# Two-layer graph-attention and mixture-of-experts kernel: x of five pairs beside layer 0's last blocks, and the last stage of tiles 0 to 11 beside layer 1's last blocks

## The chip, the core and the metric

The kernel runs on one NeuronCore of a Trainium2 chip. Its time is the device time of one execution, in microseconds. A core has five engines with a queue each: PE multiplies matrices (PEld is its loading of weights), DVE and ACT work on vectors, POOL does too and issues the indirect DMAs, and SP issues the other DMAs. All DMAs run on the core's 16 DMA engines. An engine does its instructions in their order; an instruction that waits holds up all behind it on that engine.

## The reference, cut to what matters

x has 2708 rows of 256 numbers. Each of two layers adds first an attention over the graph `adj` and then a mixture of experts, in which each row goes to its two best of 8 (layer 0) or 16 (layer 1) experts:

```python
x = x + gnn0(layernorm(x), adj)           # softmax attention over the neighbours
x = x + ffn0(layernorm(x))                # 8 experts, 256 -> 1024 -> 256, gelu, top 2
x = x + gnn1(layernorm(x), adj)           # hyperbolic attention
n = layernorm(x)
x = x + (layernorm(n + moe1(n)) * gamma + beta)   # 16 experts, 256 -> 512 -> 256, relu, top 2
```

All four parts depend on all rows of the part before, so each seam between two of them is a place where work can run dry.

## The kernel before

The rows are in 22 tiles (20 of 128 rows and two of 74), handled as 11 pairs. The kernel is one program with all loops unrolled. The orders of PE, ACT, DVE and SP are written out by the kernel itself, POOL's order is set by the compiler's scheduler.

**Experts.** In both layers the rows are sorted into blocks of 128 rows of one expert, 47 blocks in layer 0 (`SURE0`) and 45 in layer 1 (`SURE1`). For a block, SP loads the expert's w1 and w2 into one of three rooms (1 MB each in layer 0, 0.5 MB each in layer 1; a load is skipped where the room already holds the expert) and fetches the block's rows from `rows_d`. PE turns the rows (`tr_ps`), multiplies by w1 (`hid_ps`), ACT applies the function, PE multiplies by w2 (`out_ps`), DVE scales by the gate's weight (`yo`), and POOL adds the result to the rows' tokens in HBM with an indirect DMA (`add`). There are two sums in HBM, `sums[0]` for even blocks and `sums[1]` for odd ones; each add to a sum waits until the one before it on that sum has landed. `sums[0]` starts with x itself (layer 0) or its normalized rows (layer 1). Layer 0's blocks are ordered by `Experts.run`: per block it issues w1 of block b+2, the hidden products, the turn of b+1, the output of b-1, w2 of b+2, the rows of b+3, the weight of b (`weigh`: DVE `side`, ACT tanh), and then calls `beside(b)`. Layer 1's blocks are ordered by `Experts.stream`, in which generators ask a planner (`Clock`) for stretches of engine time, written as `yield "DVE", 0.7`; the planner decides by these planned times in which order the instructions are written. A `Mark` is a planned moment, `Slots` stand for a ring of buffers.

The first blocks of each layer (24 in layer 0, `EARLY0`) are full pages of the tokens of the first tiles; a page that is open then comes among the next E blocks, E being the number of experts. So all rows of the first tiles are complete after a known block.

**The seam between the layers.** After layer 0's last block, `project1` runs for each pair, paced by `Turns`: SP reads the pair's rows from both sums into `h_all` and `xp`, POOL adds them (L1468), SP keeps the sum in `x_d` for later, DVE computes mean and variance (L421, L422), ACT and DVE the root, DVE applies it (`xr`, L437), PE turns the pair (`tr_ps`, L455), ACT copies it (`xts`) and squares its rows (`norms`, L1496), PE multiplies by `w1x` (`u_ps`, L460), ACT copies the result to `h_all`. The attention of layer 1 follows.

**The end.** In layer 1, `add_beta` makes POOL add a column and beta to x1 (two operations a tile, L1854 and L1855). After the last block `load_y` reads all 22 tiles from both sums into `y_all` (which lies over `mask_t`), in the groups 2, 2, 4, 4, 4, 4, 2. `last1` adds the two sums on PE (`y_ps`, L1894), DVE computes mean and variance, ACT and DVE the root, ACT applies it (L446), and `out_rows` multiplies by gamma on POOL (L1914), adds x1 on DVE (L1918) and stores to `out`.

Of the kernel before, what the change touches and what calls it, by code (L numbers as in the profile page):

```python
# [146 lines left out]
def kernel(  # L147
# [72 lines left out]
    def row_tile(name, bufs):  # L220
        return row.tile([P, D], F32, name=name, tag=name, bufs=bufs)
# [26 lines left out]

    room_scope = ExitStack()
# [6 lines left out]
    def xn_tile():  # L256
        return keep0.tile([P, RW], F32, name="xn", bufs=4)
# [16 lines left out]

    x_all = keep0.tile([P, T, D], F32, name="x_all")
# [431 lines left out]
    class Experts:  # L707
# [5 lines left out]
        def __init__(self, layer, router, w1, b1, w2, func, sums, tags, xg, xt, bias, sure):  # L713
            self.layer, self.router, self.w1, self.w2 = layer, router, w1, w2
            self.func, self.sums, self.b1 = func, sums, b1
            self.t_tag, self.h_tag, self.o_tag = tags
            self.xg_tile, self.xt_tile, self.bias_tile = xg, xt, bias
            E, _, self.F = w1.shape
            self.FC, self.NB = self.F // P, router.blocks
            self.rooms, self.rows, self.known, self.planned, self.stages = {}, {}, 0, 0, []  # L720
            self.last_add, self.adds = {}, []
            self.b1_rows = w1x.rearrange("p c f -> p (c f)")[:E, :self.F]
            self.taken, self.sure = taken_of[layer], sure
# [177 lines left out]
        def add(self, b, yo):  # L901
            k = b % 2
            ins = nc.gpsimd.indirect_dma_start(  # L903
                out=self.sums[k][:, :], in_=yo, in_offset=None,
                out_offset=bass.IndirectOffsetOnAxis(ap=self.rows.pop(b)[:, D:D + 1].bitcast(I32),
                                                     axis=0), compute_op=OP.add)
            if k in self.last_add:
                tc.add_manual_dep(ins.ins, self.last_add[k].name, LANDED, reason="the same rows")
            self.last_add[k] = ins.ins
            if k == 0:  # L910
                self.adds.append(ins.ins)
# [6 lines left out]
        def store(self, t, r, src):  # L918

            ins = nc.sync.dma_start(self.sums[0][t * P:t * P + r, :], src)  # L920
            for other in self.adds:
                tc.declare_no_dep(ins.ins, other, reason="other tokens' rows")

# [12 lines left out]
        def stream(self, clock, stages, bank, acc, xrs, los, wides, widened, started):  # L936
# [3 lines left out]
                {upto: Mark() for upto in stages} for _ in range(3))  # L940
            hidden_at, out_at, xg_at, xt_at, ht_at, w_at = (
# [67 lines left out]
            def finish(b, ps, slot):  # L1009
                yield "DVE", 0.7  # L1010
                yo = self.scaled(b, ps, weights.pop(b))
                clock.set(slot)
                yield "POOL", 1.6
                self.add(b, yo)
                clock.set(xr_slots.pop(b))

# [213 lines left out]
    def close0(pair, ahead, behind, last=False):  # L1230
# [19 lines left out]
        for t, r in pair:  # L1250
            router0.rows[t] = keep0.tile([P, RW], F32, name="xr", bufs=5)
            ln_f0.apply(router0.rows[t][:r, :D], x_all[:r, t, :], t, r)
            yield 1
# [137 lines left out]

    with tc.tile_pool(name="experts0", bufs=1) as late0:
        room = late0.tile([P, 4096], F32, name="room2")
        experts0.add_room(2, room[:, :2048], room[:, 2048:])
        l1_weights = []

        def combine(b):
            if b == EARLY0 + 2:
                l1_weights.extend(load_combined(late0))
            if b == EARLY0 + 4:  # L1400
                combine_weights(*l1_weights)

        experts0.run(late0, turns, (2, 1, 2), combine)
# [6 lines left out]
    h_all = side.tile([P, T, D + 1], F32, name="h_all1")  # L1410
# [24 lines left out]
    ln_a1 = Norm("a1")  # L1435
    c0, scale, p_all, p_scale = kept("c0", 1.0), kept("scale"), kept("p_all"), kept("p_scale")
    norms = kept("norms", 1.0, 2 * T).rearrange("p (k t) -> p k t", k=2)

    def fetch_rows(tl, src, group):

        full = [t for t, r in group if r == P]
        if full:
            lo = full[0] * P
            nc.sync.dma_start(tl[:, :len(full)], src[lo:lo + len(full) * P, :].rearrange(  # L1444
                "(t p) d -> p t d", p=P))
        if len(full) < len(group):
            nc.sync.dma_start(tl[:TAIL, len(full):], src[TF * P:W, :].rearrange(
                "(t p) d -> p t d", p=P)[:TAIL])

    x_d = dram.tile([W, D], F32, name="x_d")  # L1450

    def keep_rows(src, pair):
        if pair[1][1] == P:
            lo = pair[0][0] * P
            nc.sync.dma_start(x_d[lo:lo + 2 * P, :].rearrange("(t p) d -> p t d", p=P), src)
        else:
            for q, (t, r) in enumerate(pair):
                nc.sync.dma_start(x_d[t * P:t * P + r, :], src[:r, q])

    def project1(pair):  # L1460

        xa = h_all[:, pair[0][0]:pair[0][0] + 2, :D]
        xb = side.tile([P, 2, D], F32, name="xp", bufs=4)
        fetch_rows(xa, sums0[0], pair)
        fetch_rows(xb, sums0[1], pair)
        yield 3
        if pair[1][1] == P:
            nc.gpsimd.tensor_tensor(xa, xa, xb, OP.add)  # L1468
        else:
            for q, (t, r) in enumerate(pair):  # L1470
                nc.gpsimd.tensor_tensor(xa[:r, q], xa[:r, q], xb[:r, q], OP.add)
# [8 lines left out]
        xp = [side.tile([P, RW], F32, name="xr", bufs=13)[:, :D] for _ in pair]  # L1480
        for q, (t, r) in enumerate(pair):
            ln_a1.apply(xp[q][:r], xa[:r, q], t, r)
        yield 1
        ps = ps_tile("tr_ps", "tr").rearrange("p (t c n) -> p t c n", c=DC, n=P)
# [10 lines left out]
        for q, (t, r) in enumerate(pair):  # L1495
            nc.scalar.activation(row_tile("junk", 4)[:r, 1:], xp[q][:r, 1:], AF.Square,  # L1496
                                 accum_out=norms[:r, 0, t:t + 1])
# [83 lines left out]
    widen(0, 1)  # L1581
    widen(1, 1)
    FIRST = 12
    for k in range(len(pairs) + 11):
        if k < len(pairs):
            turns.start(project1(pairs[k]))
        turns.step()
        if k in (12, 14):
            widen(k // 2 - 6, 0)

        if k == FIRST // 2 + 10:
            turns.start(factors1(0, FIRST))
        if k >= FIRST // 2 + 13:
            lo = 4 * (k - FIRST // 2 - 13)
            split_h(lo, lo + 4)
# [24 lines left out]
    def xr_tile():  # L1620
        return side.tile([P, RW], F32, name="xr", bufs=13)

# [13 lines left out]
    bank, acc, xrs, xps, los, xtss = (Slots(clock, n) for n in (5, 3, 13, 4, 2, 2))  # L1636
# [48 lines left out]
    def finish1(t, r):  # L1685
# [3 lines left out]
        lo, ex = (side.tile([P, D], F32, name=nm, bufs=2) for nm in ("lo", "ex"))  # L1689
# [35 lines left out]
    def points1(group):  # L1725
# [5 lines left out]
        def fetch_x():  # L1731
            for k in range(0, n, 2):
                xp_slots.append((yield from xps.get()))
                xp = side.tile([P, 2, D], F32, name="xp", bufs=4)
                fetch_rows(xp, x_d, group[k:k + 2])
                xq.extend((xp[:, 0], xp[:, 1]))
                clock.moved(x_at[k // 2], 0.9, 2.0)
# [36 lines left out]
        for q, (t, r) in enumerate(group):  # L1774
            if q % 2 == 0:
                yield x_at[q // 2]
            yield "DVE", 1.1
            nc.vector.scalar_tensor_tensor(x1[:r, t, :], emb[:r, t, :], by[:r, q:q + 1], xq[q][:r],
                                           op0=OP.mult, op1=OP.add)
            ln_f1.stats(x1[:r, t, :], t, r)  # L1780
            if q % 2:
                clock.set(xp_slots[q // 2])
# [65 lines left out]
    def add_beta(b):  # L1848
        if b == 20:
            for name, src in (("gamma", L1_ffn_gamma), ("beta", L1_ffn_beta)):  # L1850
                last[name] = broadcast_rows(name, src, 0, D, nc.sync, last["pool"])
        if 22 <= b < 22 + T:
            t, r = tiles[b - 22]
            nc.gpsimd.tensor_scalar(x1[:r, t, :], x1[:r, t, :], common[:r, t:t + 1], None, op0=OP.add)  # L1854
            nc.gpsimd.tensor_tensor(x1[:r, t, :], x1[:r, t, :], last["beta"][:r], OP.add)  # L1855

    experts1.beside = add_beta
    for t in range(2):
        clock.start(finish1(*tiles[t]), 0)
    clock.start(widener())  # L1860
    clock.start(attention(), 2)
    experts1.stream(clock, (*early1.values(), experts1.NB), bank, acc, xrs, los, wides, widened,
                    started)
    clock.run()
    experts1.rest()
    experts1_scope.close()

    psum_stage(wide=5, acc=3)
# [3 lines left out]
    clock = Clock()  # L1872
    bank = Slots(clock, 5)
# [53 lines left out]

    nc.scalar.preload_act_table_set(LN_TABLE)
    loads = [Mark() for _ in firsts]
    for group, mark in zip(firsts, loads):  # L1930
        load_y(group, mark)
    for group, mark in zip(firsts, loads):
        clock.start(last1(group, mark))
# [32 lines left out]
```

## Time and profile before

| | us |
|---|---|
| median of 3 runs | 1194.71 (1188.9 to 1196.87) |
| profiled execution | 1168.86 |
| its span, first to last instruction | 1167.1 |
| PE busy in the span | 1051.8 (90%) |
| DVE, ACT, POOL busy | 527.4, 586.5, 404.6 |
| granted PE clock, mean | 0.951 |
| layer 0's blocks end on PE | 667.3 |
| layer 1's blocks end on PE | 1115.0 |

The profile is of one execution, so its sums are to be held against 1168.86 and not against the median. In timelines a row gives start, duration, engine, line, operation, tiles and count, and in brackets how long the engine was idle before it and what ended that. Matmuls are pipelined and their ends are modelled. In windows, each engine's busy time is followed by the granted clock, the mean share of time in which the 16 DMA engines were busy, and what they moved.

### The profile page before, as it was taken

The numbers are of one execution on the slowest core, as the hardware profiler recorded it, in microseconds if no ns is written. First come the engines' busy times: TensorE is split into PE (matmuls) and PEld (weight loads), VectorE is DVE, ScalarE is ACT, GpSimd is POOL, SyncE is SP. The second block draws the span as 40 slices with busy tenths as digits, with TensorE's granted clock in tenths as the row PEclk, the third lists the DMA queues.
The fourth block names the chain that finished last, engine by engine and source line by source line (L and its number), as shares of the span: only waits on it lengthen the run. The fifth ranks groups of instructions, "written<-read, shape, count | busy, mean of one in ns | idle before, by whom it ended". The sixth has DMA issues, their size and how long they took to land. (4 is left out here: it accounts for less than half of the span.)

```text
span 1167.1 us, 21436 instructions
## 1 busy us (share of the span) xinstructions
PE 1051.8 (90%) x6753; PEld 932.8 (80%) x6753; DVE 527.4 (45%) x2024; ACT 586.5 (50%) x1637; POOL 404.6 (35%) x467
## 2 busy tenths in 40 slices
PE   5999999987999999999999859998985898999963
PEld 3788888876789999998999724898984888898852
DVE  7778888866531111111100164747778551111136
ACT  4876666654534444443444347527744543444413
POOL 7521121111142222221222261253555376384325
PEclk9999999998999999999999979999887799999987
DMA  9964445410889999999899589500224487777963
GB/s 297 297 213 161 168 149 176 135 78 27 295 276 283 314 326 323 320 291 344 260 314 321 158 270 243 176 1 7 76 82 135 121 207 193 188 206 203 251 193 111
DMA packets 163486, 238.96 MB, mean 205 GB/s; under 512 B 10415, under 2 KB 137046, under 8 KB 160658
## 3 DMA queue, kind: packets, MB, share of 16 engines
q1 hardware_dynamic: 144550, 214.09, 56.0%
q0 software_dynamic: 18816, 23.42, 10.5%
q8 instruction: 57, 0.93, 0.3%
q14 instruction: 63, 0.52, 0.1%
HBM read 205.54 MB, written 54.99 MB: 223 GB/s over the span
## 5 line engine op out<-in xcount | busy, mean ns | idle before, releaser
L898 DVE TENSOR_SCALAR yo<-out_ps,w 128x256 f32<-128x256 f32 x92 | 44.5, 483 | 422.4 <-PE out_ps L892 422.1
L1219 PE MATMUL att_ps<-g_all,z 128*128 128x257 f32 (+3 forms) x968 | 228.1, 389 | 0.0
L1219 PEld LDWEIGHTS att_ps<-g_all,z 128*128 128x128 f32 (+3 forms) x968 | 177.6, 189 | 36.4 <-issue 8.7
L892 PE MATMUL out_ps<-room,ht 128*128 128x256 f32 x872 | 201.6, 383 | 0.0
L892 PEld LDWEIGHTS out_ps<-room,ht 128*128 128x128 f32 x872 | 163.0, 193 | 21.5
L874 PEld LDWEIGHTS hid_ps<-xt,room 128*128 128x128 f32 x1504 | 174.9, 192 | 3.0 <-ACT xt L859 0.8
L874 PE MATMUL hid_ps<-xt,room 128*128 128x128 f32 x1504 | 175.9, 275 | 0.5 <-ACT xt L859 0.5
L1205 ACT ACTIVATE zr<-e_bc,minus_one,g_all 128x256 f32<-128x256 f32 (+3 forms) x242 | 130.5, 591 | 57.6 <-DVE z L1208 57.0
L903 POOL DMA_INDIRECT sums<-yo,xg x43 | 67.0, 1558 | 245.1 <-DVE side L866 208.2
L878 ACT ACTIVATE ht<-hid_ps,w_t 128x128 f32<-128x128 f32 x376 | 128.4, 364 | 22.7 <-PE hid_ps L874 3.5
L668 POOL DMA_INDIRECT rows_d<-xr,place x88 | 92.1, 1046 | 124.6 <-DVE xr L437 76.9
L1570 PE MATMUL att_ps<-half,wide_mask 128*128 128x258 f32 (+1 forms) x968 | 127.2, 294 | 2.5 <-ACT h_all L1507 1.5
L1570 PEld LDWEIGHTS att_ps<-half,wide_mask 128*128 128x128 f32 (+1 forms) x968 | 124.0, 198 | 3.9 <-ACT h_all L1507 2.4
L1208 DVE SCALAR_TENSOR_TENSOR z<-zr,mask_t 128x256 f32<-128x256 f32 (+3 forms) x242 | 97.9, 425 | 33.0 <-ACT zr L1205 18.3
L878 ACT ACTIVATE ht<-hid_ps,w1x 128x128 f32<-128x128 f32 x180 | 65.3, 365 | 92.5 <-PE hid_ps L874 87.9
L903 POOL DMA_INDIRECT sums<-yo,xr x45 | 70.1, 1558 | 78.1 <-DVE w L896 26.8
L868 ACT ACTIVATE w<-xg,side 128x1 f32<-128x1 f32 x43 | 12.7, 295 | 167.5 <-DVE side L866 167.5
L455 PE MATMUL tr_ps<-ident,xr 128*128 128x128 f32 (+1 forms) x222 | 42.1, 302 | 35.8 <-DVE xr L437 16.3
L1430 POOL CAST wide_mask<-mask_t 128x1408 fp32r<-128x1408 fp8e4 x31 | 42.5, 1379 | 83.0 <-PE att_ps L1570 83.0
L874 PE MATMUL hid_ps<-lo,wide_mask 128*128 128x128 f32 x480 | 63.9, 288 | 5.5 <-DMA wide_mask<-in_L_ffn_w_dram 5.5
L874 PEld LDWEIGHTS hid_ps<-lo,wide_mask 128*128 128x128 f32 x480 | 61.1, 202 | 8.8 <-issue 7.8
L455 PEld LDWEIGHTS tr_ps<-ident,xr 128*128 128x128 f32 (+1 forms) x222 | 30.5, 159 | 43.8 <-POOL h_all L1468 15.6
(287 smaller groups left out, 1429.6 us busy)
## 6 DMA issues: line engine op xcount, KB each, us to landing
room<-in_L_ffn_W_dram SPq DMA_DIRECT2D x94, 1024.0 KB
wide_mask<-in_L_ffn_w_dram SPq DMA_DIRECT2D x60, 512.0 KB
room<-in_adj_dram SPq DMA_DIRECT2D x20, 1354.0 KB
room<-in_L_ffn_w_dram SPq DMA_DIRECT2D x30, 512.0 KB
rows_d<-nobody SPq DMA_DIRECT2D x1, 7511.0 KB
rows_d<-nobody SPq DMA_DIRECT2D x5, 1295.0 KB
sums<-nobody SPq DMA_DIRECT2D x2, 2944.0 KB
xr<-rows_d SPq DMA_DIRECT2D x45, 129.5 KB
```

The lines of the kernel that those rows point to most:

```text
L455: nc.tensor.transpose(ps[:, c, :r], src[:, c * P:(c + 1) * P], ident[:r, :r])
L668: ins = nc.gpsimd.indirect_dma_start(out=self.rows_d[:, :], in_=self.rows[t][:r], in_offset=None, out_offset=bass.IndirectOffsetOnAxis(ap= ...
L874: nc.tensor.matmul(ps[:, :P], w1_b[:, c, f * P:(f + 1) * P], xt[:, c, :], start=(c == 0), stop=(c == DC - 1))
L878: nc.scalar.activation(ht[:, f, :], ps[:, :P], self.func, bias=self.bias[:, f, b:b + 1])
L892: nc.tensor.matmul(ps[:, :D], ht[:, f, :], self.rooms[b % 3][1][:, f, :], start=False, stop=(f == self.FC - 1))
L898: nc.vector.tensor_scalar(yo, ps[:, :D], w, None, op0=OP.mult)
L903: ins = nc.gpsimd.indirect_dma_start(out=self.sums[k][:, :], in_=yo, in_offset=None, out_offset=bass.IndirectOffsetOnAxis(ap=self.rows.pop ...
L1205: nc.scalar.activation(zr[:k, :n], e_bc[:k, lo:lo + n], AF.Relu, bias=minus_one[:k], scale=g_all[:k, j, D + 1:D + 2])
L1208: nc.vector.scalar_tensor_tensor(z[:k, :n], zr[:k, :n], 1.0, mask_t[:k, j // 2, lo:lo + n, j % 2], op0=OP.add, op1=OP.mult)
L1219: nc.tensor.matmul(accs[i][:r, :D + 1], z[:k, q * P:q * P + r], g_all[:k, j, :D + 1], start=(j == 0), stop=(j == LAST))
L1430: nc.gpsimd.tensor_copy(m, src)
L1570: nc.tensor.matmul(accs[i][:, :D + 2], wide_masks[i, j % 2][:k, j // 2, :], half_k[:k, j, :], start=(j == 0 and half_k is halves[0]), stop ...
```

## The change

**At the seam.** `h_all` and two rings of row buffers now live in a pool `lasting` that is there from the start, and `x_all` is a part of `h_all`, with rows of 257 words. A function `ahead(b)` is called beside layer 0's last blocks. After block 40 it has SP read pairs 0 to 2 from both sums, after block 41 pairs 3 and 4 (the second sum into the free tiles 12 to 21 of `h_all`), and POOL add them; these reads wait for adds of blocks before 32 alone (`early_read`). DVE computes the statistics of the ten tiles after blocks 43 and 44; after block 45 it computes the root and applies it to four pairs, and SP stores the five pairs to `x_d`; after block 46 ACT squares the four pairs' rows. Behind the last block, pair 4 is applied, and pairs 0 to 4 go straight to the turn. Pairs 5 to 10 take the old way, in `prepare1`, with one ring of 13 row buffers in place of `xr` and `xp`, single-tile reads of the second sum and single-tile adds on POOL. Later fetches of x from `x_d` use the ring `xr0` of five rows.

**At the end.** `add_beta` starts one DVE operation a tile, from block 20 on, in place of POOL's two. Tiles 0 to 5 are finished once the adds of blocks before 36 are done, tiles 6 to 11 once those before 39 are: SP reads them, POOL adds pairs, DVE does the rest. In SP's order the reads stand right behind w1 and ahead of w2 of block 40 and of block 42. Behind the last block `load_y` and `last1` handle tiles 12 to 21 alone, in groups of 2, 2, 4 and 2, and the six finished pairs are stored behind these reads.

```diff
+    lasting = mask_scope.enter_context(tc.tile_pool(name="lasting", bufs=1))
+    h_all = lasting.tile([P, T, D + 1], F32, name="h_all")
+    x_all = h_all[:, :, :D]
...
     def xn_tile():
-        return keep0.tile([P, RW], F32, name="xn", bufs=4)
+        return lasting.tile([P, RW], F32, name="xn", bufs=4)
+
+    def xr0_tile():
+        return lasting.tile([P, RW], F32, name="xr", bufs=5)
...
+        def early_read(self, k, ins, done):
+            for b, other in self.adds[k]:
+                if b >= done:
+                    tc.declare_no_dep(ins.ins, other, reason="other tokens' rows")
+            self.early_reads[k].append(ins.ins)
...
+    AHEAD = 5
+    MOST, DONE = 4 * AHEAD + E0 - 1, EARLY0 + E0
+    first, at2 = tiles[:2 * AHEAD], T - 2 * AHEAD
...
+    def ahead(b):
+        left = SURE0 - 1 - b
+        if left in (6, 5):
+            for k in range(3) if left == 6 else range(3, AHEAD):
+                for half, at in ((0, 2 * k), (1, at2 + 2 * k)):
+                    experts0.early_read(half, fetch_rows(h_all[:, at:at + 2, :D], sums0[half],
+                                                         pairs[k]), DONE)
+                xa = h_all[:, 2 * k:2 * k + 2, :D]
+                nc.gpsimd.tensor_tensor(xa, xa, h_all[:, at2 + 2 * k:at2 + 2 * k + 2, :D], OP.add)
+        if left in (3, 2):
+            for t, r in first[:6] if left == 3 else first[6:]:
+                ln_a1.stats(x_all[:, t], t, r)
+        if left == 1:
+            rsqrt(ts(ln_a1.mv[:, :2 * AHEAD, 1], LN_EPS, OP.add), ln_a1.rstd[:, :2 * AHEAD])
+            for k, pair in enumerate(pairs[:AHEAD]):
+                keep_rows(h_all[:, 2 * k:2 * k + 2, :D], pair)
+                if k < AHEAD - 1:
+                    normed[k] = [(xn_tile if k < 2 else xr0_tile)()[:, :D] for _ in pair]
+                    for xp, (t, r) in zip(normed[k], pair):
+                        ln_a1.apply(xp, x_all[:, t], t, r)
+        if left == 0:
+            for k, pair in enumerate(pairs[:AHEAD - 1]):
+                square_rows(normed[k], pair)
...
-    for k in range(len(pairs) + 11):
-        if k < len(pairs):
-            turns.start(project1(pairs[k]))
+    for k in range(AHEAD):
+        turns.start(project1(pairs[k], normed[k]), k)
+    for k in range(17):
+        if AHEAD + k < len(pairs):
+            turns.start(prepare1(pairs[AHEAD + k]))
         turns.step()
...
     def add_beta(b):
-        if 22 <= b < 22 + T:
-            t, r = tiles[b - 22]
-            nc.gpsimd.tensor_scalar(x1[:r, t, :], x1[:r, t, :], common[:r, t:t + 1], None, op0=OP.add)
-            nc.gpsimd.tensor_tensor(x1[:r, t, :], x1[:r, t, :], last["beta"][:r], OP.add)
+        if 20 <= b < 20 + T:
+            clock.start(add_to_x(*tiles[b - 20]), 3)
+
+    def add_to_x(t, r):
+        yield "DVE", 0.47
+        nc.vector.scalar_tensor_tensor(x1[:r, t, :], x1[:r, t, :], common[:r, t:t + 1],
+                                       last["beta"][:r], op0=OP.add, op1=OP.add)
...
+    EARLY_LAST = ((tiles[:6], 36), (tiles[6:12], 39))
+
+    def early_last(group, done):
+        yield experts1.added_at[done - 1]
+        mark, lo, n = Mark(), group[0][0], len(group)
+        for k in range(2):
+            experts1.early_read(k, fetch_rows(y_all[:, k, lo:lo + n], sums1[k], group), done)
+        clock.moved(mark, 0.8 * n, 2.5)
+        yield mark
+        for t in range(lo, lo + n, 2):
+            yield "POOL", 1.3
+            nc.gpsimd.tensor_tensor(y_all[:, 0, t:t + 2], y_all[:, 0, t:t + 2],
+                                    y_all[:, 1, t:t + 2], OP.add)
+        for t, r in group:
+            yield "DVE", 0.63
+            ln_y.stats(y_all[:, 0, t], t, r)
+        yield small(13)
+        rsqrt(ts(ln_y.mv[:, lo:lo + n, 1], LN_EPS, OP.add), ln_y.rstd[:, lo:lo + n])
+        for t, r in group:
+            yield "DVE", 0.95
+            y = y_all[:, 1, t]
+            nc.vector.scalar_tensor_tensor(y, y_all[:, 0, t], ln_y.mv[:, t, 0:1], last["gamma"],
+                                           op0=OP.subtract, op1=OP.mult)
+            nc.vector.scalar_tensor_tensor(y, y, ln_y.rstd[:, t:t + 1], x1[:, t, :], op0=OP.mult,
+                                           op1=OP.add)
...
-    for group, mark in zip(firsts, loads):
+    late_last = [tiles[12:14], tiles[14:16], tiles[16:20], tiles[20:22]]
+    loads = [Mark() for _ in late_last]
+    for group, mark in zip(late_last, loads):
         load_y(group, mark)
+    for group, _ in EARLY_LAST:
+        for (t, _), _ in zip(group[::2], group[1::2]):
+            nc.sync.dma_start(of_pair(out, t), y_all[:, 1, t:t + 2])
```

## The prediction

> **What bounds the kernel now.** I began with the page's busy row (PE 90%) and then looked for the stretches where PE is not busy, because a kernel at 90% can only gain there. In the timeline of PE two of them touch the change. Columns: start, us, line, what, and in brackets the idle time before and what ended it.
>
> ```profile
> 663.68 3.62 PE L892 MATMUL out_ps<-room,ht 128*128 128x256 f32 x16
> 682.50 1.09 PE L455 MATMUL tr_ps<-ident,xr 128*128 128x128 f32 x4 [15.20 <-DVE xr L437]
> 684.70 1.12 PE L455 MATMUL tr_ps<-ident,xr 128*128 128x128 f32 x4 [1.12 <-DVE xr L437]
> 685.61 5.03 PE L460 MATMUL u_ps<-w1x,xts 128*128 128x512 f32 x8
> 690.48 0.60 PE L455 MATMUL tr_ps<-ident,xr 128*128 128x128 f32 x4
> 690.91 3.60 PE L460 MATMUL u_ps<-w1x,xts 128*128 128x512 f32 x8
> ...
> 1105.61 2.02 PE L874 MATMUL hid_ps<-lo,wide_mask 128*128 128x128 f32 x16 [0.41 <-DMA wide_mask<-in_L_ffn_w_dram]
> ...
> 1113.26 1.89 PE L892 MATMUL out_ps<-room,ht 128*128 128x256 f32 x8
> 1124.49 8.49 PE L1894 MATMUL y_ps<-mask_t,ident 128*128 128x256 f32 x26 [9.33 <-DMA mask_t<-sums]
> ```
>
> The first is the seam between the layers: PE ends layer 0 at 667.3 and waits 15.2 us, because x must come back from HBM only after the last scatter-add landed (SP issues its first read at 672.1), and be added, normalized and turned. From there PE is the bound again, 3.87 us a pair (690.48 to 694.35). The second is the end: PE is done at 1115.0, and the kernel ends 52 us later. The chain that ended last says what fills this:
>
> ```profile
> 1069.45 51.82 DMA sums<-yo,xr x9
> ...
> 1124.94 8.81 DMA mask_t<-sums
> ...
> 1160.17 0.69 DVE mask_t L1918
> ```
>
> The last add lands at 1121.3 (T below), the reads follow, then DVE is nearly full with 22 tiles until the last store is issued at 1160.9, T + 39.6; 6.2 us later the span ends. What both moves lean on is the DMA engines, so the last view is the windows (after each engine's busy time come the granted clock, the DMA share and GB/s):
>
> ```profile
> 620.00:640.00 20.00, 20.00 (x145) 18.92 (x144) 2.12 (x9) 9.50 (x30) 4.67 (x3) 1.00 1.02 335
> 640.00:650.00 10.00, 10.00 (x69) 9.36 (x68) 1.36 (x5) 3.25 (x11) 1.55 (x1) 1.00 1.00 316
> 650.00:660.00 10.00, 10.00 (x78) 9.56 (x76) 0.91 (x4) 5.49 (x18) 3.11 (x2) 1.00 0.61 177
> 680.00:690.00 10.00, 6.38 (x15) 3.52 (x16) 9.34 (x34) 5.18 (x21) 6.20 (x11) 0.58 1.09 380
> ...
> 1090.00:1095.00 5.00, 5.00 (x39) 4.77 (x39) 0.67 (x3) 2.87 (x11) 2.70 (x2) 1.00 0.69 114
> 1095.00:1100.00 5.00, 5.00 (x34) 4.52 (x33) 0.67 (x3) 2.22 (x8) 1.82 (x2) 1.00 1.03 316
> 1100.00:1105.00 5.00, 4.55 (x31) 3.77 (x29) 0.67 (x3) 1.82 (x6) 1.55 (x1) 1.00 1.06 321
> ```
>
> Beside layer 0's last blocks PE and DMA are both full; DMA only falls idle at 655. So what is moved there is not free.
>
> **The seam, what goes.** Five pairs are read, added and normalized beside blocks 40 to 45. After the changed order PE can turn pair 0 right behind the last block, and the first wait is ACT's: its weight of block 46 ends at 664.7, then stand the eight moved squares (704.04 to 704.45, so 0.41 each, 3.3), 0.5 for the branch as now (664.7 to 665.2), the table load 1.28, one copy 0.6: 670.4. The first u starts there and not at 685.6. Its cold clock goes too: the row of 680:690 shows 0.58, and turn and u took 1.09, 1.12 and 5.03 instead of 0.60, 0.60 and 3.60, 2.4 us more. [...] Pair 1's u then starts at 674.4 and not at 690.9: 16.5 us, of which I take **16**. Is something else late next? Pair 5 is read as pair 0 was, first at about 672, ready for PE 10.4 us later at 682.5; PE reaches it after five pairs of 3.87, at 690. 8 us of cover, so the single-tile reads of the new ring (three DMAs a pair, some 0.45 of SP each) and POOL's adds in two halves cost nothing.
>
> **The seam, what comes.** SP issues ten reads of 262 KB, six behind block 40 and four behind block 41, ahead of the weights of blocks 43 and 44, into a full DMA: 2.62 MB. How late may weights be? Block 46's w1 was issued at 645.0, w2 at 649.3, DMA fell idle at 655.2; w2's 1.05 MB took the last 2.8 us at 380 GB/s, so w1 had landed near 652.5 to 652.8, and PE wanted it at 656.4: 3.6 us of slack. At this stage's own 335 GB/s the reads take 7.8 us, at the 380 of 680:690 (where the same reads ran) 6.9: PE loses 4.2 or 3.3. [...] The last three of POOL's five adds (1.1 to 1.26) stand in front of block 42's scatter-add and hold it some 3 us; a half has an add every 14.7 us, each landing after 6.9: nothing. DVE's ten statistics (0.6 each), one root (12 x 0.16) and eight applies (0.41) lie in its 6.2 us of idle per block; behind them waits only yo, and PE has two banks for it. The five stores of x follow when no weights are left to load. Net of the seam: 16 - 4 = **12**.
>
> **The start.** x now lives in rows of 257 words, so its loads land in 1 KB pieces. Applies from such rows took 430 ns in layer 1 against 546 for x_all in the first 90 us, so no loss on DVE; for the loads 0 to 1 us, taken as 0.
>
> **The middle.** POOL loses 44 operations on x1 (0.9 and 0.7 each); DVE gets 22 (0.47, as L1778's) over 22 blocks of 3.84 with 3.18 idle: nothing, and nothing gained: the wait at 904 hangs on DVE's numbering and 12 scatters at 1.27. The x fetch has two slots instead of four; rows of tile 17 then wait for tile 12's use at 889, are there at about 892 and wanted at 895.
>
> **The end, what goes.** Tiles 12 to 21 remain: 2.6 MB to read instead of 5.8. The first bn stays at T + 7.0, the first POOL product at T + 11.6 (1132.9). The last tiles land near T + 11 (2.6 MB at 340 behind 3.2 of latency), bn near T + 15; ten POOL products at 0.95 end near T + 21. DVE has ten bn pairs (0.61), five adds (0.9) and four roots (1.6): 17 us from T + 7. I take the last store at T + 22.5 instead of T + 39.6: **17**. The six early stores (1.6 MB) run behind the reads and before the late ones.
>
> **The end, what comes.** Two groups of reads, 1.57 MB each, stand on SP ahead of w2 of blocks 40 and 42. Group one waits for block 35's add (issued at 1081.0, landing 5.3 later as the last add did, 1116.0 to 1121.3; SP gets there at 1088: no wait). Group two waits for block 38's, issued at 1093.7, so SP stands from 1097 to about 1099, and behind it w2 of 42 and all of 43. Of 3.15 MB, 1090 to 1094 takes 0.94 (84 GB/s used of 320); 2.2 MB at 320 come out as 6.9 us ahead of block 43's weights, for which PE already waits (0.41). No cover; PE's last blocks are late by about **6.5**, between 0 and 10. DVE's added work (12 x 0.61, two roots, 24 x 0.45, some 22 us) nearly fills its idle time behind block 40 and waits for POOL, which waits for the reads: side of 41 and so ACT may be held up to 3 us, inside the same stall. Net: 17 - 6.5 = **10.5**.
>
> **Sum.** 12 + 10.5 = 22.5: the profiled execution's 1168.86 becomes 1146. The median of the runs shown is 1194.71, 26 us above the profile, which the trace doesn't explain; I carry the gain over in microseconds: **1172**.
>
> **Rivals.**
> *The backlog is paid in full* (chance 0.25): both inserts cost their bytes, 8 and 10, and 16 - 8 + 17 - 10 = 15 gives 1180. For it: shares over 1.0, and the slower runs may be slow through DMA. Against it: the slack of 3.6 and the hole at 1090.
> *The cover holds* (0.20): no stall in either place, 33 us, 1162. For it: DMA ran at 380 to 400 for microseconds; against it: PE already waits for weights at 1101 and 1105.
> *Slower* (0.03): the early reads crawl beside weights and scatter-adds and SP stands before the weights. Of the 5.77 MB the hole at 1090 takes 0.94; the other 4.83, less 3.6 us of slack in layer 0, eat the 33 us once they move below 132 GB/s (36.6 us); at 95 they cost 47, and the kernel is 14 us slower, 1209. Against it: the same reads ran at 380, and at 339 to 366 between 1126 and 1138.
> *The early reads don't start early* (0.02): if they waited for all adds, nothing would move, 1195. The changed order shows the ten first ones waiting for queue slots alone.
> The forecast itself: 0.50.
>
> **Range and chances.** Run medians can tell 1% here, 12 us. The range goes from the covered case, 1160, to beyond the paid one with a late ACT, 1187. Faster: 0.49 of the forecast, 0.20, and 0.16 of the paid case, 0.85; slower 0.03; within 1% 0.12.
>
> **What would show it.** Right: PE's gap at the seam under 4 us at clock 1.0; waits for room of 1 to 3 us each before blocks 43 and 44 of layer 0; a wait of some 6 us before block 43 of layer 1; T to the last store 22 to 23. Wrong: the turn of pair 5 waiting for DVE, or a tail that still takes 30 us because DVE slows beside POOL.

## The result, and the profile after

| | before | after |
|---|---|---|
| median, us | 1191.89 (16 runs, 1186.3 to 1197.1) | 1181.69 (16 runs, 1175.82 to 1186.6) |
| ratio, 95% interval | | 0.9908 (0.9889 to 0.9928) |
| profiled execution, us | 1168.86 | 1183.92 |
| its span, us | 1167.1 | 1182.2 |

The kernel is 0.9% faster, 10.2 us by the medians, where 22.5 us were forecast. The profiled execution of before was some 23 us quicker than the median of before, that of after was not, so the two spans must not be subtracted: each stretch is compared by itself and, for the whole, with a second profile of before that is shown below.

The timeline of PE after the change, at the same places as before (start, us, what; in brackets the idle time before it and what ended that):

```profile
637.18 3.81 PE L880 MATMUL hid_ps<-xt,room 128*128 128x128 f32 x32 [1.80 <-DMA room<-in_L_ffn_W_dram]
646.42 3.81 PE L880 MATMUL hid_ps<-xt,room 128*128 128x128 f32 x32 [1.65 <-DMA room<-in_L_ffn_W_dram]
...
668.45 3.62 PE L898 MATMUL out_ps<-room,ht 128*128 128x256 f32 x16
673.14 1.06 PE L461 MATMUL tr_ps<-ident,xn 128*128 128x128 f32 x8 [1.07 <-DVEq L943]
674.79 3.67 PE L466 MATMUL u_ps<-w1x,xts 128*128 128x512 f32 x8 [0.58 <-ACT xts L1557]
678.30 0.60 PE L461 MATMUL tr_ps<-ident,xr 128*128 128x128 f32 x4
678.73 3.60 PE L466 MATMUL u_ps<-w1x,xts 128*128 128x512 f32 x8
...
1126.68 3.75 PE L880 MATMUL hid_ps<-lo,wide_mask 128*128 128x128 f32 x16 [6.88 <-DMA wide_mask<-in_L_ffn_w_dram]
...
1137.02 1.89 PE L898 MATMUL out_ps<-room,ht 128*128 128x256 f32 x8
1149.09 5.92 PE L1981 MATMUL y_ps<-mask_t,ident 128*128 128x256 f32 x18 [10.18 <-DMA mask_t<-sums]
1155.58 1.56 PE L1981 MATMUL y_ps<-mask_t,ident 128*128 128x256 f32 x6 [0.57 <-DMA mask_t<-sums]
1158.72 0.65 PE L1981 MATMUL y_ps<-mask_t,ident 74*74 74x256 f32 x2 [1.58 <-DMA mask_t<-sums]
1161.89 5.45 PE L1981 MATMUL y_ps<-mask_t,ident 74*74 74x256 f32 x14 [2.51 <-DMA mask_t<-sums]
```

The seam has changed as forecast: the gap of 15.2 us is gone, two waits for weights of 1.80 and 1.65 us have come before blocks 43 and 44 of layer 0, and the first projection starts at 674.79 instead of 685.61. At the end two things stand out: 6.88 us of waiting before block 43 of layer 1, with its hidden product at half speed behind it (3.75 us where 1.95 is usual), and two waits late in the tail (1.58 and 2.51 us), before the matmuls of the last two tiles, which have 74 rows. The windows show the same two inserts from the side of the DMA engines (busy time of each engine, granted clock, DMA share, GB/s):

```profile
630.00:640.00 10.00, 8.20 (x59) 7.45 (x58) 0.76 (x3) 4.02 (x12) 5.77 (x5) 1.00 1.08 371
640.00:650.00 10.00, 8.35 (x60) 7.60 (x60) 3.62 (x15) 4.09 (x13) 4.61 (x4) 1.00 1.08 379
...
680.00:690.00 10.00, 10.00 (x31) 4.86 (x30) 3.63 (x10) 5.83 (x23) 6.68 (x11) 1.00 0.83 275
1115.00:1120.00 5.00, 4.29 (x28) 3.54 (x27) 4.42 (x21) 1.01 (x4) 0.85 (x2) 1.00 0.94 300
1120.00:1125.00 5.00, 0.00 (x0) 0.00 (x0) 4.83 (x10) 1.32 (x5) 3.26 (x3) 0.70 1.10 355
1125.00:1130.00 5.00, 3.32 (x15) 3.35 (x16) 4.77 (x13) 1.33 (x4) 3.87 (x3) 0.50 0.33 59
```

From 1120 to 1125 PE does nothing and DMA is full: the reads of tiles 6 to 11 and the weights behind them. In the next 5 us PE runs at a granted clock of 0.50. The chain that ended last names the second place:

```profile
1119.48 26.52 DMA sums<-yo,xr
...
1149.54 12.30 DMA mask_t<-sums
1161.84 0.04 issue
1161.89 5.46 PE y_ps L1981 x14
...
1175.45 0.69 DVE mask_t L2005
```

The read of the last two tiles from the second sum is issued at 1149.54 and takes 12.30 us to land. T, the moment at which SP can issue the first late read, is 1146.07 here. The last store is issued at 1176.2, T + 30.1, where before had T + 39.6 and T + 22.5 was forecast.

### The profile page after: what moved, and what is told of

Same layout as the page of the kernel before. It is cut to its first block, busy times and chain, and to the rows that moved or that the text cites. A ratio compares the mean times of both kernels' runs of the same rounds, so it can differ in the third digit from the quotient of the medians.

```text
span 1182.2 us, 21323 instructions
## 1 busy us (share of the span) xinstructions
PE 1049.9 (89%) x6705; PEld 928.9 (79%) x6705; DVE 537.3 (45%) x2073; ACT 575.6 (49%) x1609; POOL 367.1 (31%) x422
## 3 DMA queue, kind: packets, MB, share of 16 engines
q0 software_dynamic: 18816, 23.42, 10.4%
## 5 line engine op out<-in xcount | busy, mean ns | idle before, releaser
L898 PE MATMUL out_ps<-room,ht 128*128 128x256 f32 x872 | 199.0, 380 | 0.0
L884 ACT ACTIVATE ht<-hid_ps,w_t 128x128 f32<-128x128 f32 x376 | 128.4, 364 | 30.8 <-PE hid_ps L880 8.2
L884 ACT ACTIVATE ht<-hid_ps,w1x 128x128 f32<-128x128 f32 x180 | 61.3, 362 | 97.7 <-PE hid_ps L880 82.0
L880 PE MATMUL hid_ps<-lo,wide_mask 128*128 128x128 f32 x480 | 67.3, 298 | 15.2 <-DMA wide_mask<-in_L_ffn_w_dram 13.7
L880 PEld LDWEIGHTS hid_ps<-lo,wide_mask 128*128 128x128 f32 x480 | 64.5, 211 | 19.3 <-issue 15.5
L898 PE MATMUL out_ps<-wide_mask,ht 128*128 128x256 f32 x240 | 61.3, 401 | 0.0
L461 PE MATMUL tr_ps<-ident,xr 128*128 128x128 f32 (+1 forms) x214 | 38.8, 290 | 23.9 <-DMA xr<-rows_d 9.0
```

What stands on the lines that cost most here:

```text
L461: nc.tensor.transpose(ps[:, c, :r], src[:, c * P:(c + 1) * P], ident[:r, :r])
L880: nc.tensor.matmul(ps[:, :P], w1_b[:, c, f * P:(f + 1) * P], xt[:, c, :], start=(c == 0), stop=(c == DC - 1))
L884: nc.scalar.activation(ht[:, f, :], ps[:, :P], self.func, bias=self.bias[:, f, b:b + 1])
L898: nc.tensor.matmul(ps[:, :D], ht[:, f, :], self.rooms[b % 3][1][:, f, :], start=False, stop=(f == self.FC - 1))
```

## Experiments

### Is the profile of before typical, and does the one of after repeat?

Both kernels were profiled again, unchanged.

> The kernel before, profiled once more. The profiled execution of before took 1168.9 us, while its timed runs took 1186 to 1197. If that execution was only an unusually quick one, this one lies near 1190 us and shows where the 20 us sit: theory A says in layer 1 between 890 us and block 40 (stretches that wait for DMA or for late semaphores), with the seam (gap of some 15 us on the matmul engine before the first projection of layer 1) and the end (last store some 40 us after the last add has landed) unchanged. Theory B says that the seam and the end are themselves shorter or longer by several us from one execution to the next, so that the sums made from one profile do not hold.

> The changed kernel, profiled once more. Theory A (the seam pays about 10.5 us in every execution, the end pays nothing): matmuls of layer 0 end about 4 us later than before, the first projection of layer 1 starts some 11 us earlier, the matmul engine stands 6 to 8 us before block 43 of layer 1 again, the two loads of the last two tiles' rows land 9 to 12 us after their issue again, and the last store is issued about 30 us after the last add has landed. Theory B (an accident of one execution): the stall before block 43 is under 3 us or the last store is issued within 25 us of the last add.

Measured: 1192.87 and 1185.76 us for one execution each. The landmarks, in us:

| | before | before, again | after | after, again |
|---|---|---|---|---|
| first hidden product of layer 1 starts | 905.4 | 916.2 | 901.5 | 907.1 |
| hidden product of block 44 starts | 1109.5 | 1133.6 | 1133.3 | 1136.9 |
| T | 1121.3 | 1145.4 | 1146.1 | 1149.5 |
| last store, after T | 39.6 | 39.5 | 30.1 | 28.5 |
| end of the span | 1167.1 | 1191.1 | 1182.2 | 1184.0 |

The seam and the end of before are what they were: here is its second profile at the seam, on PE.

```profile
683.65 1.08 PE L455 MATMUL tr_ps<-ident,xr 128*128 128x128 f32 x4 [13.86 <-DMA xp<-sums]
687.11 1.12 PE L455 MATMUL tr_ps<-ident,xr 128*128 128x128 f32 x4 [2.38 <-DVE xr L437]
688.02 4.63 PE L460 MATMUL u_ps<-w1x,xts 128*128 128x512 f32 x8
```

The 24 us between the two profiles of before lie elsewhere: 11 us come up to the first hidden product of layer 1, another 13 from there to block 44. In the second profile's table of waits (engine, line, what ended it: total, times, longest, in us) stand rows that the first profile has not at all:

```profile
ACT where L829 <- remote: 14.0, 2, 11.5
DVE inv L1692 <- remote: 10.3, 1, 10.3
ACT w1x L850 <- remote: 9.7, 1, 9.7
```

They are told of in the last section; they belong to both kernels alike, so theory A stands and B falls. For the change, this says two things. Against a like profile, after keeps what the seam gave until layer 1's first block (916.2 to 907.1: 9.1 us). And the end takes about as much as it gives: in the second pair of profiles the time from the start of block 40's hidden product to that of block 44's is 26.4 us instead of 16.1, and from T to the last store 28.5 instead of 39.5.

### Each half alone

The seam alone, all 22 tiles' last stage as before:

```diff
-    EARLY_LAST = ((tiles[:6], 36), (tiles[6:12], 39))
+    EARLY_LAST = ()
-    late_last = [tiles[12:14], tiles[14:16], tiles[16:20], tiles[20:22]]
+    late_last = firsts
```

> The change without its last part: no tile's last stage runs beside layer 1's blocks, all 22 tiles are done after them as before. By the sum on record the seam alone gives 16 - 4 = 12 us: about 1180 us against 1192. By theory A, from the trace of after (first projection at 674.8 instead of 685.6 us, stall of 3.5 us in layer 0 already paid), it gives 10 to 11 us, all of the gain measured for the whole change. By a third theory (the middle gives the seam's gain back, since the first block of layer 1 started only 3.7 us earlier in the trace of after), it gives 4 us or less.

The end alone is the kernel before with `early_read`, `early_last`, `add_to_x` and the late part of the change put in, and nothing of `ahead`.

> The kernel before with only the last part of the change: tiles 0 to 11 have their last stage beside layer 1's last blocks, and x1 is completed on the vector engine from block 20; the seam is as before. By the sum on record it gives 17 - 6.5 = 10.5 us. By theory A it gives 0 (within 2 us): in the trace of after the matmuls of blocks 42 to 44 lost 9.2 us against before, and the stretch from the last add's landing to the end shrank by 9.6 us, not 17. By the third theory (the seam's gain is given back) it must give 6 us or more, since the whole change gives 10.

Measured against before, beside both: the seam alone 0.9902 (0.9867 to 0.9938), the end alone 1.0011 (0.9995 to 1.0027). So **the seam gives all of the gain**, about 11 us, and the end gives nothing, which is theory A; neither the sum on record (12 and 10.5) nor the third theory fits. PE in the profile of the seam alone, and, behind the line of dots, of the end alone:

```profile
641.84 3.81 PE L880 MATMUL hid_ps<-xt,room 128*128 128x128 f32 x32 [1.50 <-DMA room<-in_L_ffn_W_dram]
651.98 5.44 PE L880 MATMUL hid_ps<-xt,room 128*128 128x128 f32 x32 [2.55 <-DMA room<-in_L_ffn_W_dram]
680.34 1.06 PE L461 MATMUL tr_ps<-ident,xn 128*128 128x128 f32 x8 [1.07 <-DVEq L943]
...
1140.02 3.72 PE L874 MATMUL hid_ps<-lo,wide_mask 128*128 128x128 f32 x16 [6.69 <-DMA wide_mask<-in_L_ffn_w_dram]
```

The wait before block 43 comes with the end part alone, and is 6.69 us. Its last store is at T + 31.1, that of the seam alone at T + 39.2. In the seam alone the second wait in layer 0 is 2.55 us, and the hidden product behind it takes 5.44 us instead of 3.73: the granted clock is 0.50 for 3.41 us there (652.9 to 656.3).

### What eats the end's gain

Two suspects: the reads of tiles 6 to 11 in front of the weights, and the load of the last two tiles. Each was changed alone, then both. First, the reads of the second group wait until the last weights are issued:

```diff
         yield experts1.added_at[done - 1]
+        if done > 36:
+            yield experts1.loaded          # set by the loader behind its last block
```

> The changed kernel, with the early reads of tiles 6 to 11 (1.57 MB) put behind the weights of the last block instead of between the weights of block 42. Theory A (these reads, not those of tiles 0 to 5, make the matmul engine stand before block 43: 6.9 us in the trace of after, 7.4 in its second profile, and 2 to 3 us more at the halved clock that follows): the stall before block 43 falls under 1 us, the last add lands about 9 us earlier, and the whole is 6 to 9 us faster than after, since the work on tiles 6 to 11 now ends beside the last loads: about 1176 us against 1195 of before in the last session, ratio 0.984. Rival (the stall comes from the reads of both groups or from the stand of SP's queue behind an add): 3 us or less of it goes.

Second, the 74 rows of the last two tiles are read as 64 and 10:

```diff
+                for a, z in ((0, 64), (64, TAIL)):
+                    nc.sync.dma_start(y_all[a:z, k, lo:lo + len(group)], src[a:z])
-            fetch_rows(y_all[:, k, lo:lo + len(group)], sums1[k], group)
```

> The changed kernel, with the late load of the last two tiles, 74 rows each, taken in two pieces of 64 and 10 rows for either half of the sums, in the same place. Theory A (a DMA of 74 rows is done in 3 parts where one of 128 rows is done in 16; the two loads landed 9.6 and 12.3 us after issue in the trace of after, and the matmul engine stood 4 us for them with tiles 18 and 19 queued behind): they land within 5 us, and the last store is issued 3 to 6 us earlier than the 30 us after the last add's landing: ratio 0.994 to 0.998 below that of after. Rival (the row count does not matter, the queue is just full): landing within 1 us of before, no gain.

Third, both edits:

> Both edits together: the reads of tiles 6 to 11 behind the last weights, and the last two tiles' load in pieces of 64 and 10 rows. Theory A: the sum of the two, 9 to 14 us faster than after, about 1172 us, ratio to before near 0.981. If they overlap (the last stage of tiles 6 to 11, now later, is what ends last), 7 to 9 us only.

| | median, us | ratio to before (95%) | wait before block 43 | T to last store |
|---|---|---|---|---|
| after | 1181.69 | 0.9908 (0.9889 to 0.9928) | 6.88 | 30.1 |
| group 2 behind the weights | 1175.50 | 0.9865 (0.9834 to 0.9895) | none | 29.2 |
| tail rows in two pieces | 1175.77 | 0.9878 (0.9845 to 0.9911) | 7.19 | 24.6 |
| both | 1177.73 | 0.9876 (0.9846 to 0.9907) | none | 30.8 |

In the profiles each edit removes what it was aimed at. With group 2 behind the weights the wait before block 43 is gone, though the reads of tiles 0 to 5 still stand where they stood: so it was group 2. Group 1 seems not to be free either: a wait for weights stands before block 41 in nine of the eleven profiles with its reads (1.1 to 1.7 us, once 3.2; not in the first profile of after and not in that of the end alone), and in none of the three without them. With the tail rows in pieces the loads land 5.3 to 8.0 us after issue instead of 9.6 and 12.3, the last of them at T + 11.5 instead of T + 15.8, PE no longer stops for them, and the last store moves up by 5.5 us. (That profile is of the quickest of its six runs, 1167.52 us, so only this stretch of it is compared.) PE in the tail with the pieces:

```profile
1138.05 7.03 PE L1986 MATMUL y_ps<-mask_t,ident 128*128 128x256 f32 x18 [10.08 <-DMA mask_t<-sums]
1145.92 5.02 PE L1986 MATMUL y_ps<-mask_t,ident 128*128 128x256 f32 x22 [0.84 <-DMA mask_t<-sums]
```

But they don't add up. By the ratios to before the first gave some 5 us where 9 of waiting and half clock went, and the second 3.6 of its 5.5; the intervals of all four overlap, so that in the times neither step is clear of the noise. The profile of group 2 behind the weights shows why for the first:

```profile
1115.15 2.02 PE L880 MATMUL hid_ps<-lo,room 128*128 128x128 f32 x16 [1.11 <-DMA room<-in_L_ffn_w_dram]
...
1126.95 2.05 PE L880 MATMUL hid_ps<-lo,room 128*128 128x128 f32 x16
...
1130.79 1.89 PE L898 MATMUL out_ps<-room,ht 128*128 128x256 f32 x8
1149.64 10.48 PE L1984 MATMUL y_ps<-mask_t,ident 128*128 128x256 f32 x40 [16.96 <-DVEq L943]
```

PE waits 16.96 us for DVE to pass the branch behind the last block (L943), and in DVE's order its work on tiles 6 to 11 stands ahead of that branch: it now runs from 1137.7 to 1149.2, while both halves of the first late tiles had landed by 1144. That work, on the critical path now, takes the place of the wait removed. A smaller part: beside these 1.57 MB of reads the adds of blocks 40 and 41 landed 6.9 and 6.8 us after issue, the last three 3.9 to 5.0.

### Less at the seam, too

On top of both edits, pairs 3 and 4 are read behind the last weights of layer 0:

```diff
-        if left in (6, 5):
+        if left in (6, 2):
```

and their statistics, root and apply stand behind the last block.

> As the one before, and at the seam only pairs 0 to 2 (1.57 MB) are read ahead of the last weights of layer 0; pairs 3 and 4 (1.05 MB) are read behind them, and their normalisation stands after the last block. By the price that the seam's reads had (3.1 to 3.5 us of stall for 2.62 MB, of which the slack of the weights covers some 3.6 us of transfer), the stall falls to 0.5 us or less and 2.5 to 3 us are gained on top. Rival: the normalisation of pairs 3 and 4 on the vector engine (some 6 us) comes late for their projection and takes it back: no gain, or a loss of up to 3 us.

Measured: 1174.71 us, ratio 0.9845 (0.9815 to 0.9874). One wait of 1.83 us is left at the seam instead of two with 3.5 to 4, so the slack covers less than I had reckoned (in the trace of before the last weights of block 46 landed at 653.5, and not at the 652.5 to 652.8 of the prediction, so it was 3.0 us and not 3.6); the projections of pairs 3 and 4 start without a wait, so the rival is out. The gain over the kernel with both edits, 3 us by the medians, is within the intervals; against after, whose interval (0.9889 to 0.9928) lies wholly above, this version is faster.

### Is the second group worth having?

Three ways to treat tiles 6 to 11, all built on the last kernel (both edits, and less at the seam; ratio 0.9845). First, they are read behind the weights, but their last stage runs in the schedule of the late tiles (`last1`), not in `early_last`; then the same with four tiles; then no second group at all (6 tiles early, 16 late).

```diff
         clock.moved(mark, 0.8 * n, 2.5)
+        if done > 36:
+            return
...
+    for group in [tiles[6:8], tiles[8:12]]:
+        clock.start(last1(group, there))
```

> As the last kernel of the call before (late reads of tiles 6 to 11, tail rows in pieces, pairs 3 and 4 read behind the last weights), but the last stage of tiles 6 to 11, once read, is no longer done by GpSimd and the vector engine ahead of the late tiles: it goes through the same path as the late tiles (matmul engine, vector, scalar, GpSimd), in their schedule. Theory A (in that kernel the matmul engine waited 17 to 18 us after the last block, until the vector engine had ended its 11 us of work on tiles 6 to 11 at 7 us after the late loads had begun to land): the first late matmul starts within 4 us of the last block's end, and 4 to 8 us are gained: 1167 to 1171 us where that kernel had 1174.7 and before 1192.2, ratio to before 0.979 to 0.982. Rival (the landing of the last adds, slowed by the reads ahead of them in the queues from 3.7 to 8 us, sets the end): 2 us or less.

> The same with four tiles (6 to 9, 1.05 MB) read behind the last weights in place of six. If the reads ahead of the last adds are what delays these (adds of blocks 40 to 42 landed 7 to 8 us after issue where 3.7 is usual), the last add lands 1.5 to 3 us earlier and this one is faster by up to 1 us in spite of 0.52 MB more to load after it; if the loads after the last add set the end (10 tiles, 2.6 MB, in some 8 us), it is slower by 1 to 2 us.

> As the kernel with late reads of tiles 6 to 11 (tail rows in pieces, pairs 3 and 4 of the seam read behind the last weights; ratio 0.9845 to before), but tiles 6 to 11 have no early part at all: 6 tiles early, 16 tiles late. If the second group was worth something once its reads stood behind the weights, this is slower than 0.9845 by the 6 tiles' share of the late work, 6 x 0.8 us of loads or 4 to 6 us (ratio 0.988 to 0.990). If it was worth nothing (its vector work stood before the late tiles and its reads slowed the last adds by 3 us), the ratio is 0.983 to 0.986. There is no stall over 2.5 us at a read of the early tiles in layer 1 in either case.

Measured: 0.9866 (0.9839 to 0.9893), 0.9865 (0.9842 to 0.9888) and 0.9848 (0.9819 to 0.9878). In the first, PE's late matmuls do start at once, 2.11 us after the last block:

```profile
1115.05 5.38 PE L1995 MATMUL y_ps<-mask_t,ident 128*128 128x256 f32 x16 [2.11 <-PEq L943]
1124.46 11.00 PE L1995 MATMUL y_ps<-mask_t,ident 128*128 128x256 f32 x40 [4.04 <-DMA mask_t<-sums]
```

and yet nothing is won. T is 1121.74, 14.5 us after block 44's hidden product started, and the last store is at T + 28.0: these matmuls end early, but the work of ACT, POOL and DVE on tiles 6 to 11 now lies behind the last block too. With four tiles T comes 12.1 us after the start of block 44's hidden product, as expected for fewer reads beside the adds, and the last store at T + 30.1. Without the second group these are 13.6 us and T + 33.9, and the one wait for weights before the last blocks is that of 1.45 us before block 41. The ratios of the three and of the kernel that they are built on lie between 0.9845 and 0.9866 with intervals that overlap: the second group is worth nothing that these runs can show, however it is placed. The first two of the three ran beside a before of 1169 us, the third beside one of 1199, so only ratios can be compared.

### Waits beside the scatters

> The changed kernel with four small fills (0.2 us each) put on GpSimd after the two scatters of each tile of layer 1; nothing else moves. In seven of the eight profiles looked at, the matmul engine's signals reached nobody for 12 to 14 us while GpSimd issued 12 scatters back to back (15 us), and came 1 to 2 us after the last one; in the first profile of before they came at once. Theory C (a back-to-back run of scatters holds the signals up): with fills between the pairs signals come through after each pair, the longest gap falls to 4 us or less, and 3 to 10 us are gained. Rival (the hold-up has another cause): the gap stays at 11 us or more, and the 0.8 us x 6 longer run of scatters costs up to 5 us.

Measured: ratio 1.0094 (1.0071 to 1.0116). The run tells nothing of its question, for two reasons. The scheduler moved all 88 fills to the start of the program, 18.6 to 55.1 us, so the scatters still ran back to back. And in this group no profile shows these waits. The loss, about 21 us against what after would have taken there (0.9908 of 1169), is close to the 20.6 us that the 88 fills take on POOL (234 ns each); that they are the whole of it was not looked into.

## Why the prediction was right and wrong

The forecast was 1172 us, within 1160 to 1187, by a gain of 22.5 us; 10.2 us came. That 1181.69 lies within the range is no merit of the sum: the range was wide enough for the rivals too, and half of the sum, the end, came to nothing. Step by step:

**The seam, what goes: right.** First projection forecast at 670.4, or 674.4 with the stall; measured 674.79, gaps of 1.07 and 0.58 us. That PE would run at its full clock there was an estimate; the granted clock was 1.00 from 667 to 690. Pair 5's turn waited for nothing.

**The seam, what comes: right.** Forecast 4 us, waits of 1 to 3 us before blocks 43 and 44; measured 1.80 + 1.65 = 3.45, and 3.1 to 4.1 in the other profiles with the same reads. The 4 itself was an estimate between the 4.2 and 3.3 reckoned from two windows of before. One cost was not priced: in three of these profiles (the seam alone, group 2 behind the weights, both edits) the second wait was 2.2 to 2.6 us, and the product behind it took 5.44 instead of 3.73 us, at a granted clock of 0.50. The shortest of these waits was 2.15 us. In the windows DMA moved 371 and 379 GB/s there, within the 335 to 380 that I had taken from the windows of before. Net 12 forecast at the second pair's projection; 12.2 there in the trace of after (690.91 to 678.73), 10.8 at the first pair's, about 11 by the times of the seam alone.

**The start and the middle: right.** Both at nothing: the seam alone keeps its lead over the second profile of before from layer 1's first hidden product (10.4 us earlier) to T (10.3) and the end (10.8). At the first projection it led by 6.0; where the rest came in between was not looked into.

**The end, what goes: wrong**, 17 us forecast, 9.5 measured (T + 39.6 to T + 30.1). The step that failed is "the last tiles land near T + 11": it divided bytes by a rate, as if all reads moved at one rate. (The bytes were a little too many as well, since the 74-row tiles were counted as full: 2.4 MB remain of 5.5, not 2.6 of 5.8.) The reads of 74 rows were slower. Each landed in 3 steps where one of 128 rows landed in 16, and the two, 0.15 MB each, took 9.6 and 12.3 us, the later one landing at T + 15.8. From 1155.6 to 1156.8, when the other late reads had landed, DMA moved 48 GB/s at a share of 0.13, about what two of the 16 engines make; tiles 18 and 19 stood behind on PE, whose granted clock was 0.50 from 1160 to 1164. The trace of before shows the same reads landing 10.0 and 11.8 us after issue, hidden behind 20 other tiles; I had looked at who waited, not at how long they took, and with 12 tiles gone the cover was gone. The five stores of early pairs behind the first show the same: 14 of their 16 steps land 2.1 to 3.2 us after issue, the last two 5.3 to 6.8, as if two engines were still at the 74 rows. With the pieces the last store was at T + 24.6, so this is 5.5 of the 7.6 us missed. Of the other 2.1 some stand in the sum itself: 17 us of DVE from T + 7 end at T + 24, not at T + 22.5. The rest was not looked into.

**The end, what comes: mechanism right, size wrong**, 6.5 forecast, 10.2 measured. The wait before block 43 was 6.88 and made up as forecast, from bytes and from SP's stand for an add (2.2 us, 1110.98 to 1113.18), here in SP's order:

```profile
1110.61 0.37 SPq L749 DMA_DIRECT2D wide_mask<-in_L_ffn_w_dram  x1
1113.18 0.96 SPq L1417 DMA_DIRECT2D mask_t<-sums  x2
1114.55 0.54 SPq L753 DMA_DIRECT2D wide_mask<-in_L_ffn_w_dram  x1
```

Left out were the half clock behind such a wait (block 43's hidden product, and the turn and output that follow it, took 2.7 us longer; I had priced this at the seam and not here), and 1.0 us by which the last add's landing came later still behind block 44. From the start of block 40's hidden product to that of 44 it is 25.94 instead of 16.76 us, 9.2 more; with the 1.0 this makes the 10.2. Why the last add landed later was not looked into.

So the end came to 9.5 - 10.2, with 0.2 us less behind the last store: nothing, as the end alone shows. Of the rivals, "the backlog is paid in full" came nearest in its number, 1180, but not in its reason: at the seam the backlog cost 3.5 us and not 8, and what was overrated was the tail's gain. "The early reads don't start early" and "slower" are out by the traces.

**The base.** I noted 26 us between the profile and the median and carried microseconds over. That held: the 24 us lie in stretches that the change doesn't touch. (The median of 16 runs was 1191.89, 2.8 below the base of 1194.71.)

## What to carry to other kernels

When work is taken out of a tail, list what it covered, with the duration of each item and not only with who waits for it: a slow transfer that nobody waits for today is the next bound. In these runs what was read early into a stage whose DMA engines were full was paid for by its bytes, less the slack of what stood behind it (waits of 3.45 us for 2.62 MB at the seam, of 6.88 us at the end), and by the clock where the wait grew long (0.50 behind the 6.88 us); behind the stage's last weights it was free on that side, but then the work on it must not stand, in any engine's order, ahead of what ends last. Where a gain is the sum of several parts, run each part alone: here half of the change carried all of it.

## What the runs showed of the hardware

**Long waits beside a row of scatters.** Where the kernels ran beside a before of 1192 to 1199 us, all ten profiles show waits of 7 to 12 us by ACT and DVE for products of PE, while POOL issues a row of indirect scatters, 12 of them in 15 us. In the profile of after, the two products of `where_ps` end on PE at 878.1, the scatters end at 886.8, and ACT takes the products up at 889.0 ("remote" is a wait whose cause the profile can't name):

```profile
ACT where L835 <- remote: 11.4, 1, 11.4
ACT w1x L856 <- remote: 11.0, 1, 11.0
DVE inv L1758 <- remote: 8.9, 1, 8.9
```

In the group with a before of 1169 us, and in the first profile of before, also 1169, such rows are missing altogether: in that profile of before PE ends the same products at 888.1 and ACT takes them up at 888.2, while the 12 scatters run on to 897.3. It is not the chip: a group with 1192 and the group with 1169 ran on the same one. The expectation above puts the wait down to PE's signals alone. The trace lists none of these between 874.7 and 887.5, but it lists only 3 of the 20 that DVE's instructions should have left in that stretch either, and over the whole run 92 to 94% of DVE's in the ten profiles and all of them in the four others. So the trace is short of records where the waits are, and a missing record is no proof of a late signal. That the waits go with the longer times is shown; what causes them is open.

**The clock of PE.** Behind waits of 1.93 us (after, layer 1, at 1097.9), 2.15, 2.35 and 2.55 us (layer 0, the profiles named above) the granted clock fell to 0.50, each time for 3.41 us; behind the waits of 1.80 and 1.65 us of after in layer 0 it stayed at 1.00. The length of the wait alone does not settle it: behind one of 2.21 us in layer 1 (group 2 behind the weights, at 1102.3) the hidden product took 2.02 us, where 1.95 is usual and 3.59 came behind the 1.93 us.

**Row counts.** Apart from the pieces above, single-tile reads of after show the same: 74 rows of 1 KB took 4.1 and 6.1 us to land at 911, 128 rows issued just before took 2.1. So does the store of the last pair in the same profile, issued at 1172.26 with no other transfer under way: 74 rows landed after 5.2 us in 3 steps (35 GB/s at a DMA share of 0.13 from 1173.5 to 1174.8), the pair of 128 rows before it after 2.0 in 16.

**Landing of adds.** An indirect add landed 3.7 to 3.8 us after issue with no other transfer under way (the last three of before), and 6.8 and 6.9 us after it beside 1.57 MB of reads (blocks 40 and 41 with group 2 behind the weights); without the second group the same two took 4.6 and 4.0.
